# adj_resnorm on one core: x loaded once in eighths behind the first block of adj, its natural order made on TensorE in step 7

## The chip, the core and the metric

The kernel runs on one core of a Trainium2 chip. The metric is the device time of one execution, in microseconds (us); the median of three runs of the kernel before is 233.75 us (233.69 to 233.84). A separate execution was profiled, and all durations below are from it.

## The reference

There are 4096 nodes with 64 features each (x) and a 4096 x 4096 matrix adj of zeros and ones, both fp32. Two graph layers are applied, each followed by a residual sum and a layer norm.

```python
x = layernorm(x + L0(x, adj)); x = layernorm(x + L1(x, adj))
# L0: w = mask * 0.5 ** (k - pos): each neighbour weighted by its rank from the right, at most 100 of them
out = w @ (x @ weight) + bias
# L1: deg = rowsum(adj) + 1
z = concat([x, (adj @ x + x) / deg]) @ W + b
out = relu(z) / max(norm(relu(z)), 1e-12)
```

The rank of a neighbour is a running count along the row of adj (a cumulative sum), and the weights of layer 0 are powers of two of it.

## The kernel before, in words

adj is passed transposed and cut into 64 blocks of 512 rows of output by 512 neighbours: eight slabs g of rows, and in each eight blocks k of neighbours, taken from k = 7 down to 0. One such block is one step, numbered i = 8g + (7 - k) in the first slabs. A block is loaded by one DMA of POOL's queue, which turns fp32 into bf16 on the way (`load_next`, L102 to L110); eight loads are issued at the start and one more in each step, so that step i issues load i + 8. POOL waits in that instruction when eight loads are under way.

What a step does, in the order in which it is written (loop at L711): ACT's and POOL's planned work and `load_next`; `count` of the next step's block (L321, four column-tiled matmuls per block that count neighbours), whose sum DVE puts into `cs` (L331, L333); `weigh` of this step's block (L351 and L360, each sixteen 32x32-tiled matmuls into two PSUM buffers `v`), whose results ACT (L367) and DVE (L368) turn into the weights `w`; up to four sums of layer 1 for slabs whose input is ready (L387); `spread` (L339 on PE, then `near` on ACT, L341), which prepares the next step's counts; `gather` (L378, four matmuls that apply w of the step before to x). On each engine instructions run in the order in which they are written: the scheduler is manual for all engines, and the lists `hooks` and `PLACES` say which helper is put at which step and engine.

The two `v` buffers are the only ones of their pool: `weigh` of a step can begin to write when ACT and DVE have read those of the step before.

x is needed in two orders. The first order ("quads", tensor x_quads: partition = quarter e and place, column = block and q) is that of the neighbours. It lies in `xp`, which is the same memory as `c1`. `split_x` takes block k of it apart in step 7 - k into an fp16 high part (ACT for k = 7 and 6, L221, else POOL) and a rest (`xr`, POOL, L223), which DVE scales into the low part (L226, `split_x_low`) at the end of the step. `gather` and `early_px` read the fp16 parts. The second, natural order (tensor x, 128 rows to a partition block) is needed for the residual: `add_b0` (L311, POOL) adds the bias to `x1`, and `first_y` (L544) or `half_y` (L510) reads it when a slab's layer 0 ends, for slab 0 in step 9.

Before, x_quads is loaded as two halves of 512 KB on the SP queue ahead of and beside the first load of adj (L124), and x is loaded from memory a second time, 128 KB for each slab in step 8g + 3 (L128), each behind a small POOL memset that holds the trigger back (L127). The weights are loaded by the SP queue in step 1 behind a DVE memset (L213, L214), and POOL first uses them in step 5 (L229).

At the start PE runs 14 matmuls on zeros (L694) and later some on the first adj block (`warm`, L700) between the first count, spread and weigh. DVE and ACT build the constants from `dist`: `ident`, `has` and `past` (for `further`, L703 to L705), `mine` (L177, L179) and `tri` (L183, L184).

Of the kernel before, what the change touches and what calls it, by code (L numbers as in the profile page):

```python
# [9 lines left out]
F32 = mybir.dt.float32  # L10
BF16 = mybir.dt.bfloat16
# [4 lines left out]
ALU = mybir.AluOpType  # L16
# [4 lines left out]
POOL = mybir.EngineType.Pool  # L21
SP = mybir.EngineType.SP

P = 128
R = 512
TB = R // P
KB = 4
Q = P // 4
MAX_NEIGH = 100
STEP = 128.0  # L30
# [9 lines left out]
LAG = 1  # L40
SAVED = (15, 17, 18, 21, 27)
# [3 lines left out]
def adj_resnorm_kernel(  # L45
    ctx: ExitStack,
    tc: tile.TileContext,
    x: bass.AP,
# [20 lines left out]
    nc = tc.nc  # L69
    D = x.shape[2]  # L70
# [31 lines left out]
    def load_next(n=1):  # L102
        for _ in range(n):
            s = next(loads, None)
            if s is None:
                return
            g, k = s
            a = a16p.tile([P, KB, R], BF16, tag="a16", name=f"a16_{g}_{k}")
            nc.gpsimd.dma_start(out=a, in_=adjT[g, k])  # L109
            A[g][k] = a  # L110
# [11 lines left out]
    def load_xp(k0, k1):  # L122
        bs = slice(k0 * KB, k1 * KB)
        nc.sync.dma_start(out=xp[:, bs, :], in_=x_quads[:, bs, :])  # L124

    def load_x(g):
        nc.gpsimd.memset(x1[:, g * TB, 0:1], 0.0)  # L127
        nc.sync.dma_start(out=x1[:, ts(g, TB), :], in_=x[:, ts(g, TB), :])  # L128


    load_xp(NK // 2, NK)
    load_next()
    load_xp(0, NK // 2)
# [8 lines left out]
    load_next(6)  # L142
# [20 lines left out]
    nc.vector.tensor_scalar(cen, ident[0:D, 0:D], -1.0 / D, None, ALU.add)  # L163


# [8 lines left out]
    for e in range(4):  # L174
        one_hot = ident[quarters[e], quarters[e]].unsqueeze(2).to_broadcast([Q, 4 * NK, Q])
        if e % 2:
            nc.scalar.mul(mine[quarters[e]], one_hot, STEP)  # L177
        else:
            nc.vector.tensor_scalar(mine[quarters[e]], one_hot, STEP, None, ALU.mult)  # L179

    tri = const.tile([P, Q], BF16, name="tri")
    for rows in quarters:
        nc.vector.tensor_scalar(tri[rows], dist[rows, rows], 0.0, -STEP, ALU.is_lt, ALU.mult)  # L183
        nc.vector.scalar_tensor_tensor(  # L184
            tri[rows], ident[rows, rows], STEP * MAX_NEIGH, tri[rows], ALU.mult, ALU.add
        )
# [20 lines left out]
    nc.vector.tensor_copy(ident16, ident)  # L207
    ident_b = const.tile([P, P], BF16, name="ident_b")
    nc.vector.tensor_copy(ident_b, ident)
# [92 lines left out]
    def add_self(g):  # L302

        for q in range(TB):
            d = A[g][g][:, q, ts(q, P)]
            nc.gpsimd.tensor_tensor(d, d, ident_b, ALU.add)  # L306

# [300 lines left out]
    def at(i, engine, fn, *args):  # L608
        i, engine = PLACES.get(" ".join([fn.__name__, *map(str, args)]), (i, engine))
        hooks[i, engine].append((fn, args))  # L610

    def run(i, engine):
        for fn, args in hooks.pop((i, engine), []):
            fn(*args)
# [5 lines left out]
    for k in range(NK):  # L620
        i = when[0, k]
        at(i, POOL, split_x, k)
        at(i, DVE, split_x_low, k)
    at(1, DVE, load_weights)
# [3 lines left out]
    for g in range(NG):  # L628
        at(NK * g + 3, POOL, load_x, g)
        at(NK * g + 7, POOL, add_b0, g)  # L630
        at(min(NK * g + 12, NS - 2), POOL, add_self, g)
# [61 lines left out]
    for i in range(14):  # L693
        nc.tensor.matmul(pi, lhsT=idle[:, 0:P], rhs=idle, start=True, stop=True)  # L694

    def warm(n):

        a = A[0][NK - 1][:, 0, :]
        for i in range(n):
            nc.tensor.matmul(pi, lhsT=a[:, 0:P], rhs=a, start=True, stop=True)  # L700
# [6 lines left out]
    warm(4)  # L707
    spread(0, NK - 1)
    warm(2)
    held = None  # L710
    for c, chunk in enumerate(chunks):  # L711
        ahead = chunks[c + 1] if c + 1 < len(chunks) else []

        shares = [[]] * (len(chunk) - 1) + [ahead]
        nr = near[chunk[0][0]]
        for (g, k), share in zip(chunk, shares):
            i = when[g, k]
            run(i, ACT)
            load_next()
            run(i, POOL)  # L720

            w = weigh(g, k, nr) if i == 0 else None
            for s in share:
                count(*s, s == ahead[0], s == ahead[-1])
            run(i, "DVE, early")
            w = w or weigh(g, k, nr)
            run(i, "ACT, late")
            if i == 0:
                warm(4)
            n_todo = len(todo)  # L730
            done = some_sums(i, 0 if i in SAVED else QUOTA)
            half = 0
            if share and share[-1] == ahead[-1]:
                if held is not None and len(todo) == n_todo:

                    half = KB // 2
                    gather(*held, 0, half)
                spread(*ahead[-1])
            if i == 0:
                warm(3)  # L740
            if done is not None:
                evict_part(done)
            if held is not None:
                gather(*held, half)
            held = (g, k, w)
            if g > 0 and k == NK - 1:
                first_hT(g - 1)
            run(i, PE)
            run(i, DVE)
# [280 lines left out]
_INS = ["x", "x_quads", "adjT", "weights"]  # L1030
# [37 lines left out]
```

## Time and profile before

| what | value |
|---|---|
| median of three runs | 233.75 us |
| profiled execution | 233.72 us, of which 231.7 us are the span of the trace |
| PE busy | 209.5 us (90%) |
| DVE, ACT, POOL busy | 182.2, 140.6, 112.3 us |
| adj loads (64, 512 KB each as bf16) | 15.2 us median from issue to landing |
| x_quads (2 of 512 KB) | 4.5 us median |
| x, natural (8 of 128 KB) | 7.2 us median |
| weights (192.5 KB) | 7.2 us |

Times in the timeline count from the start of the span. In the timeline a row gives the start, the duration, the engine, the line, what is written and read, how many instructions were merged, and in brackets how long the engine had been idle and what ended that. PEld is the weight load of PE. In the row of groups the last two numbers are the idle time of the engine before the group and who ended most of it.

### The profile page before, as it was taken

What the parts mean: (1) busy time and instruction counts of PE and PEld (TensorE: products, weight loads), DVE (VectorE), ACT (ScalarE), POOL (GpSimd) and SP (SyncE); (2) the same over time, 40 slices, a digit from 0 to 9 for tenths busy, and PEclk for the clock granted to TensorE, in tenths of its full rate; (3) what the DMA queues carried; (4) which work ended last, traced back from release to release, by engine and by line L of the source; (5) the groups of instructions that cost most, each with busy time, mean ns of one, the idle gap of its engine ahead of it and who ended that gap; (6) DMA issues with size and microseconds to landing.
All of it is one profiled execution on the core that took longest, in us unless ns stands there. A gap on an engine that the chain in (4) does not pass through costs nothing.

```text
span 231.7 us, 7494 instructions
## 1 busy us (share of the span) xinstructions
PE 209.5 (90%) x3138; PEld 95.2 (41%) x3178; DVE 182.2 (79%) x454; ACT 140.6 (61%) x212; POOL 112.3 (48%) x211
## 2 busy tenths in 40 slices
PE   7589999998998999999999999999999999999910
PEld 2133445443533443334333433443334344776810
DVE  6459877997797789798975996687678866599983
ACT  6057886687778767686557455664675451142684
POOL 7439677761537081641584056325433040079970
PEclk9799999999999999999999999999999999999975
DMA  6999999999999999999999999999970000000013
GB/s 201 209 213 219 215 216 213 217 217 214 215 219 212 214 214 223 211 214 214 218 217 207 200 183 210 204 195 181 205 168 4 3 0 0 3 0 1 23 45 113
DMA packets 11984, 37.36 MB, mean 161 GB/s; under 512 B 1328, under 2 KB 3504, under 8 KB 11952
## 3 DMA queue, kind: packets, MB, share of 16 engines
q0 software_dynamic: 9216, 33.56, 73.7%
q1 hardware_dynamic: 2736, 3.34, 4.7%
q8 instruction: 24, 0.39, 0.6%
q14 instruction: 8, 0.07, 0.1%
HBM read 69.40 MB, written 1.05 MB: 304 GB/s over the span
## 4 chain that ended last, share of the span: by engine, by line
PE 40%; DVE 11%; POOL 4%; ACT 3%; issue 2%; ACTq 0%; DVEq 0%; POOLq 0%
PE acc L378 12%; PE acc_part L387 11%; PE v L351 5%; PE cnt L321 3%; PE v L360 3%; ACT u L961 2%; POOL scratch L947 2%; DVE w L368 2%; POOL scratch L978 2%; DVE cs L331 1%; PE rep L339 1%; PE va L930 1%; PE pz L505 1%; PE vb L387 1%; DVE part L403 1%
## 5 line engine op out<-in xcount | busy, mean ns | idle before, releaser
L367 ACT ACTIVATE w<-v,less 128x1024 int16<-128x1024 f32 x64 | 71.3, 1113 | 43.7 <-PE v L360 31.7
L368 DVE TENSOR_SCALAR w<-v 128x1024 int16<-128x1024 f32 x64 | 78.2, 1221 | 13.0 <-PE v L360 12.1
L378 PE MATMUL acc<-w,xhl 128*128 128x512 bf16 x235 | 65.2, 380 | 1.9 <-issue 1.1
L109 POOL DMA_DIRECT2D a<-in_adjT_dram x64 | 36.9, 622 | 48.2 <-PE acc_part L387 25.4
L387 PE MATMUL acc_part<-a,x1hl 128*128 128x512 bf16 x140 | 38.2, 381 | 1.8 <-issue 1.3
L378 PEld LDWEIGHTS <-xhl 128*128 128x128 f16 x256 | 23.1, 98 | 33.6 <-issue 9.7
L341 ACT ACTIVATE near<-rep,most 128x512 bf16<-128x512 f32 x40 | 27.3, 682 | 8.7 <-PE rep L339 8.6
L387 PEld LDWEIGHTS <-x1hl 128*128 128x128 f16 x224 | 18.6, 98 | 31.1 <-issue 13.3
L351 PE MATMUL v<-a,tri 32*32 32x512 bf16 x1024 | 29.6, 384 | 0.3 <-DVE w L368 0.2
L360 PE MATMUL v<-near,mine 32*32 32x512 bf16 x1024 | 28.1, 376 | 0.0
L331 DVE TENSOR_TENSOR cs<-cnt,cs 128x512 bf16<-128x512 f32 x32 | 21.9, 686 | 4.4 <-PE cnt L321 4.0
L321 PE MATMUL cnt<-a,pick 128*32 128x512 bf16 x256 | 21.4, 389 | 4.2 <-DMA a<-in_adjT_dram 2.9
L351 PEld LDWEIGHTS <-tri 32*32 32x32 bf16 x1024 | 9.5, 87 | 21.7 <-issue 21.5
L339 PE MATMUL rep<-cs,further 128*128 128x512 bf16 x40 | 15.4, 385 | 1.5 <-DVE cs L331 1.1
L565 POOL TENSOR_SCALAR x<-y,mv_l,r_l 128x64 f32<-128x64 f32 x16 | 9.1, 575 | 12.4 <-DVE dr L516 6.4
L947 POOL TENSOR_TENSOR scratch<-scratch,power 128x4 f32<-128x4 f32 (+1 forms) x5 | 6.4, 1279 | 15.2 <-DVE scratch L949 15.1
L306 POOL TENSOR_TENSOR a<-a,ident_b 128x128 bf16<-128x128 bf16 x32 | 12.7, 431 | 0.1
L321 PEld LDWEIGHTS <-pick 128*32 128x32 bf16 x256 | 5.9, 94 | 14.8 <-issue 11.3
L333 DVE CAST cs<-cnt 128x512 bf16<-128x512 f32 x8 | 5.5, 692 | 7.8 <-PE cnt L321 7.8
L360 PEld LDWEIGHTS <-mine 32*32 32x32 bf16 x1024 | 10.2, 87 | 2.8 <-issue 2.4
L961 ACT ACTIVATE u<-u,scratch 128x64 f32<-128x64 f32 x27 | 9.8, 428 | 2.2 <-POOL scratch L980 2.1
L944 ACT ACTIVATE u<-u 128x256 f32<-128x256 f32 (+1 forms) x5 | 2.5, 502 | 12.1 <-DVE u L933 12.1
(177 smaller groups left out, 272.2 us busy)
## 6 DMA issues: line engine op xcount, KB each, us to landing
a<-in_adjT_dram POOLq DMA_DIRECT2D x64, 512.0 KB, 15.2
c<-in_x_quads_dram SPq DMA_DIRECT2D x2, 512.0 KB, 4.5
x<-in_x_dram SPq DMA_DIRECT2D x8, 128.0 KB, 7.2
out_dram<-u SPq DMA_DIRECT2D x8, 128.0 KB, 1.7
wts<-in_weights_dram SPq DMA_DIRECT2D x1, 192.5 KB, 7.2
```

What stands on the lines that cost most here:

```text
L109: nc.gpsimd.dma_start(out=a, in_=adjT[g, k])
L321: nc.tensor.matmul(cnt[g][quarters[q], :], lhsT=pick[:, PW - 4 * k : PW - 4 * k + Q], rhs=A[g][k][:, q, :], start=first, stop=last,)
L331: nc.vector.tensor_tensor(new, cnt[g], cs[g], ALU.add)
L339: nc.tensor.matmul(pr, lhsT=further, rhs=cs[g], start=True, stop=True)
L341: nc.scalar.activation(near[g], pr, AF.Relu, bias=most, scale=-1.0)
L351: nc.tensor.matmul(v[e // 2][quarters[q], e % 2, :], lhsT=tri[quarters[e], :], rhs=A[g][k][quarters[e], q, :], start=True, stop=False,)
L360: nc.tensor.matmul(v[e // 2][quarters[q], e % 2, :], lhsT=mine[quarters[e], 4 * k + q, :], rhs=nr[quarters[e], :], start=False, stop=True,)
L367: nc.scalar.activation(w[:, 0:2, :], v[0], AF.Relu, bias=less)
L368: nc.vector.tensor_scalar(w[:, 2:4, :], v[1], -STEP * MAX_NEIGH, 0.0, ALU.add, ALU.max)
L378: nc.tensor.matmul(acc0[g], lhsT=xhl[:, b, :], rhs=w[:, q, :].bitcast(BF16), start=(k, q) == (NK - 1, 0), stop=(k, q) == (0, KB - 1),)
L387: nc.tensor.matmul(acc, lhsT=x1hl[:, b, :], rhs=A[g][b // KB][:, b % KB, :], start=first, stop=last)
L961: nc.scalar.activation(o[:, t, :], y[:, t, :], AF.Identity, bias=off[:, t : t + 1], scale=r[:, t : t + 1])
```

## The change

x is loaded once, only in the quads order, as eight blocks of 128 KB. The first adj load is issued ahead of them; block 7 follows at once, blocks 6 and 5 after the fifth and seventh adj loads, each behind a POOL memset, and blocks 4 to 0 in steps 0 to 4, on POOL's list behind `split_x` of that step. The natural order is made in step 7 by a new function, `natural_x`: sixteen fp32 matmuls, each of which multiplies a 32-row quarter of xp (512 columns) by a 32-wide identity `eye` and puts it at another quarter of partitions. They go into the two `v` buffers; ACT copies one of them and DVE the other into `x1`. In that step `gather` of the step before follows directly after, whole, ahead of `weigh`, and does not stand behind it as in other steps. `add_b0` of slab 0 moves from step 7 to step 8.

At the start 8 instead of 14 matmuls on zeros are run, and 1, 2, 3, 3 instead of 4, 2, 4, 3 on the first block. `tri` is built ahead of `has` and `past`; ACT makes three of the four parts of `mine` instead of two; `cen`, `ident16`, `ident_b` and the new `eye` are made behind the first `cs`.

```diff
--- before.py
+++ after.py
@@ -38,6 +38,8 @@
 HALVED = range(2, 7)
...
 LAG = 1
+WARM = 8, 1, 2, 3, 3
+NATURAL = 7
 SAVED = (15, 17, 18, 21, 27)
 
 
@@ -45,7 +47,6 @@
 def adj_resnorm_kernel(
     ctx: ExitStack,
     tc: tile.TileContext,
-    x: bass.AP,
     x_quads: bass.AP,
     adjT: bass.AP,
     weights: bass.AP,
@@ -67,7 +68,7 @@
 
 
     nc = tc.nc
-    D = x.shape[2]
+    D = x_quads.shape[2]
     NG, NK = adjT.shape[0], adjT.shape[1]
     NB = NK * KB
     NS = NG * NK
@@ -119,18 +120,14 @@
     prep = a16p.tile([P, KB * R // 2], F32, tag="a16", name="prep")
     xTs = [a16p.tile([P, KB, R], FP16, tag="a16", name=f"xT_{j}") for j in range(2)]
 
-    def load_xp(k0, k1):
-        bs = slice(k0 * KB, k1 * KB)
+    def load_xp(k, held=True):
+        bs = ts(k, KB)
+        if held:
+            nc.gpsimd.memset(xp[:, k * KB, 0:1], 0.0)
         nc.sync.dma_start(out=xp[:, bs, :], in_=x_quads[:, bs, :])
 
-    def load_x(g):
-        nc.gpsimd.memset(x1[:, g * TB, 0:1], 0.0)
-        nc.sync.dma_start(out=x1[:, ts(g, TB), :], in_=x[:, ts(g, TB), :])
-
-
-    load_xp(NK // 2, NK)
     load_next()
-    load_xp(0, NK // 2)
+    load_xp(NK - 1, False)
     dist = epi.tile([P, P], I32, tag="hT", name="dist")
     nc.gpsimd.iota(dist, [[1, P]], base=0, channel_multiplier=-1)
     load_next()
@@ -139,7 +136,11 @@
     nc.gpsimd.iota(of_p, [[4, KB], [4 * KB, NK], [1, 4]], base=0, channel_multiplier=-1)
     of_m = epi.tile([P, P], I32, tag="z", name="of_m")
     nc.gpsimd.iota(of_m, [[1, 4], [4 * KB, NK], [4, KB]], base=0, channel_multiplier=-1)
-    load_next(6)
+    load_next(3)
+    load_xp(NK - 2)
+    load_next(2)
+    load_xp(NK - 3)
+    load_next()
 
     idle = epi.tile([P, R], BF16, tag="near", name="idle")
     nc.vector.memset(idle, 0.0)
@@ -160,30 +161,29 @@
     nc.vector.tensor_scalar(ident, dist, 0.0, None, ALU.is_equal)
     cen, wcf, b0T = prep[0:D, 0:D], prep[0:D, D : 2 * D], prep[0:D, 2 * D : 4 * D]
     w32, wc32 = prep[:, 4 * D : 6 * D], prep[:, 6 * D : 7 * D]
-    nc.vector.tensor_scalar(cen, ident[0:D, 0:D], -1.0 / D, None, ALU.add)
-
-
-    has = epi.tile([P, P], BF16, tag="y", name="has")
-    nc.vector.tensor_scalar(has, of_p, 0.0, None, ALU.is_equal)
-    past = epi.tile([P, P], BF16, tag="hT", name="past")
-    nc.vector.tensor_scalar(past, of_m, 0.0, None, ALU.is_lt)
-
-    nc.scalar.activation(zero, zero, AF.Sqrt)
-
-    mine = const.tile([P, 4 * NK, Q], BF16, name="mine")
-    for e in range(4):
-        one_hot = ident[quarters[e], quarters[e]].unsqueeze(2).to_broadcast([Q, 4 * NK, Q])
-        if e % 2:
-            nc.scalar.mul(mine[quarters[e]], one_hot, STEP)
-        else:
-            nc.vector.tensor_scalar(mine[quarters[e]], one_hot, STEP, None, ALU.mult)
 
     tri = const.tile([P, Q], BF16, name="tri")
+    eye = const.tile([P, Q], F32, name="eye")
     for rows in quarters:
         nc.vector.tensor_scalar(tri[rows], dist[rows, rows], 0.0, -STEP, ALU.is_lt, ALU.mult)
         nc.vector.scalar_tensor_tensor(
             tri[rows], ident[rows, rows], STEP * MAX_NEIGH, tri[rows], ALU.mult, ALU.add
         )
+    has = epi.tile([P, P], BF16, tag="y", name="has")
+    nc.vector.tensor_scalar(has, of_p, 0.0, None, ALU.is_equal)
+    past = epi.tile([P, P], BF16, tag="hT", name="past")
+    nc.vector.tensor_scalar(past, of_m, 0.0, None, ALU.is_lt)
+
+    nc.scalar.activation(zero, zero, AF.Sqrt)
+
+    mine = const.tile([P, 4 * NK, Q], BF16, name="mine")
+    for e in range(4):
+        one_hot = ident[quarters[e], quarters[e]].unsqueeze(2).to_broadcast([Q, 4 * NK, Q])
+        if e:
+            nc.scalar.mul(mine[quarters[e]], one_hot, STEP)
+        else:
+            nc.vector.tensor_scalar(mine[quarters[e]], one_hot, STEP, None, ALU.mult)
+
     most = const.tile([P, 1], F32, name="most")
     nc.vector.memset(most, MAX_NEIGH)
     less = const.tile([P, 1], F32, name="less")
@@ -204,9 +204,7 @@
     nc.vector.memset(power, -0.5)
     x1T = const.tile([P, R], FP16, name="x1T")
     ident16 = const.tile([P, P], FP16, name="ident16")
-    nc.vector.tensor_copy(ident16, ident)
     ident_b = const.tile([P, P], BF16, name="ident_b")
-    nc.vector.tensor_copy(ident_b, ident)
 
     def load_weights():
 
@@ -304,6 +302,23 @@
         for q in range(TB):
             d = A[g][g][:, q, ts(q, P)]
             nc.gpsimd.tensor_tensor(d, d, ident_b, ALU.add)
+
+    def natural_x():
+
+        v = [ps_v.tile([P, 2, NK, D], F32, tag="v", name=f"xn_{i}") for i in range(2)]
+        quads = xp.rearrange("p (k e) m -> p k e m", e=4)
+        for q in range(KB):
+            for e in range(4):
+                nc.tensor.matmul(
+                    v[q // 2][quarters[e], q % 2, :, :],
+                    lhsT=eye[quarters[q], :],
+                    rhs=quads[quarters[q], :, e, :],
+                    start=True,
+                    stop=True,
+                )
+        to = x1.rearrange("p (k q) m -> p q k m", q=KB)
+        nc.scalar.copy(to[:, 0:2], v[0])
+        nc.vector.tensor_copy(to[:, 2:4], v[1])
 
     def add_b0(g):
 
@@ -621,13 +636,14 @@
         i = when[0, k]
         at(i, POOL, split_x, k)
         at(i, DVE, split_x_low, k)
+    for k in range(NK - 3):
+        at(NK - 4 - k, POOL, load_xp, k)
     at(1, DVE, load_weights)
     at(NK - 2, POOL, prepare)
     at(NK + 1, POOL, prepare_wx)
     at(NK + 2, POOL, prepare_wn)
     for g in range(NG):
-        at(NK * g + 3, POOL, load_x, g)
-        at(NK * g + 7, POOL, add_b0, g)
+        at(max(NK * g + 7, NATURAL + 1), POOL, add_b0, g)
         at(min(NK * g + 12, NS - 2), POOL, add_self, g)
     if HALVED:
         all_at(
@@ -690,7 +706,7 @@
 
 
     pi = ps_a.tile([P, R], F32, tag="acc1", name="pi")
-    for i in range(14):
+    for i in range(WARM[0]):
         nc.tensor.matmul(pi, lhsT=idle[:, 0:P], rhs=idle, start=True, stop=True)
 
     def warm(n):
@@ -704,9 +720,14 @@
     further = const.tile([P, P], BF16, name="further")
     nc.vector.tensor_copy(further, pf)
     count(0, NK - 1, True, True)
-    warm(4)
+    warm(WARM[1])
     spread(0, NK - 1)
-    warm(2)
+    warm(WARM[2])
+    nc.vector.tensor_scalar(cen, ident[0:D, 0:D], -1.0 / D, None, ALU.add)
+    nc.vector.tensor_copy(ident16, ident)
+    nc.vector.tensor_copy(ident_b, ident)
+    for rows in quarters:
+        nc.vector.tensor_copy(eye[rows], ident[rows, rows])
     held = None
     for c, chunk in enumerate(chunks):
         ahead = chunks[c + 1] if c + 1 < len(chunks) else []
@@ -723,24 +744,29 @@
             for s in share:
                 count(*s, s == ahead[0], s == ahead[-1])
             run(i, "DVE, early")
+            early = 0
+            if i == NATURAL:
+                natural_x()
+                early = KB
+                gather(*held)
             w = w or weigh(g, k, nr)
             run(i, "ACT, late")
             if i == 0:
-                warm(4)
+                warm(WARM[3])
             n_todo = len(todo)
             done = some_sums(i, 0 if i in SAVED else QUOTA)
             half = 0
             if share and share[-1] == ahead[-1]:
-                if held is not None and len(todo) == n_todo:
+                if held is not None and len(todo) == n_todo and not early:
 
                     half = KB // 2
                     gather(*held, 0, half)
                 spread(*ahead[-1])
             if i == 0:
-                warm(3)
+                warm(WARM[4])
             if done is not None:
                 evict_part(done)
-            if held is not None:
+            if held is not None and not early:
                 gather(*held, half)
             held = (g, k, w)
             if g > 0 and k == NK - 1:
@@ -1027,7 +1053,7 @@
         work.pop(name)()
 
 
-_INS = ["x", "x_quads", "adjT", "weights"]
+_INS = ["x_quads", "adjT", "weights"]
 
 
 def kernel(**inputs):
@@ -1040,8 +1066,7 @@
 
     a = np.asarray(arrays.pop("adj")).reshape(n // R, R, n // (KB * P), KB, P)
     arrays["adjT"] = a.transpose(0, 2, 4, 3, 1)
-    v = np.asarray(inputs["x"])
-    arrays["x"] = v.reshape(n // P, P, d).transpose(1, 0, 2)
+    v = np.asarray(arrays.pop("x"))
 
     v = v.reshape(n // (4 * P), 4, 4, P // 4, d)
     arrays["x_quads"] = v.transpose(1, 3, 0, 2, 4).reshape(P, n // P, d)
```

## Prediction

> **What bounds the kernel now.** I first asked where TensorE waits, in the profile's slices and in the table of waits, because a change of loads and start-up can only pay where the loads set the pace.
>
> ```profile
> PE   7589999998998999999999999999999999999910
> ...
> DMA  6999999999999999999999999999970000000013
> ```
>
> The DMA engines are full from 6 to 174 us, yet PE is over 90% busy too. The waits (total us, times, longest) decide between them:
>
> ```profile
> PE cnt L321 <- DMA a<-in_adjT_dram: 2.9, 2, 2.7
> ...
> PEld L321 <- DMA a<-in_adjT_dram: 1.0, 3, 0.4
> ```
>
> In 231.7 us PE waits 3 to 4 us for adj. The timeline says where: once for the first block (2.67 us, until 8.94), then for adj loads 7, 8 and 10, which are counted in steps 6, 7 and 9:
>
> ```profile
> 27.87 0.10 PEld L321 LDWEIGHTS <-pick 128*32 128x32 bf16 x4 [0.45 <-DMA a<-in_adjT_dram]
> ...
> 30.62 0.23 PEld L321 LDWEIGHTS <-pick 128*32 128x32 bf16 x4 [0.17 <-DMA a<-in_adjT_dram]
> ...
> 35.88 0.10 PEld L321 LDWEIGHTS <-pick 128*32 128x32 bf16 x4 [0.42 <-DMA a<-in_adjT_dram]
> ```
>
> So the kernel has two parts. Up to about 36 us, loads and engines run neck and neck; after that PE never waits for a load, and the chain that ended last is almost all PE from 90 to 190 us. What arrives at 36 us late or early is carried to the end one for one.
>
> The issue-to-landing times of single adj loads give the landings: load 0 at 1.23+7.7=8.93, load 1 at 2.31+9.1=11.4, load 2 at 3.65+10.2=13.85, load 4 at 4.9+13.9=18.8. Hence 2.45 us per load. Load 8, issued at 9.18, is the one that matters:
>
> ```profile
> DMA to landing us min/median/max: 21.4/21.4/21.4
> ```
>
> 9.18+21.4=30.6. Between loads 4 and 8 lie 11.8 us, 2.0 more than 4x2.45: the price of the weights and the first block of x, in flight then. Loads 13 (42.9) and 18 (55.6) are 12.7 apart with one 128 KB block of x between: 12.7-12.25=0.45 us per block. So the weights cost about 1.55.
>
> **The change, part by part.**
>
> *The start.* adj no longer queues behind 1 MB of x. Load 0 landed at 8.93. Bounds for it now: minus the 1 MB at its measured peak (the 4.0 to 5.0 us slices move about 420 GB/s: 2.5 us), plus one block (0.45), is 6.9; minus eight blocks at 0.45 plus one is 5.8. I take 6.4. Fewer warming matmuls, tri ahead of has and past, and the casts moved behind the first cs let PE follow 2 to 2.5 us earlier. If the clock starts cold that costs under 1 us, hidden as shown next.
>
> *What becomes of that gain.* The x taken out of the front comes back between the adj loads. Until load 8 lands: 8 loads, seven blocks of x, the weights: 6.4 + 8x2.45 + 7x0.45 + 1.55 = **30.7 us, against 30.6 before**. Only one block (the first natural one) is really gone by then. The engines run at 2.3 us a step (counts at 18.07, 20.34, 22.89, 25.21) and would reach step 7 at about 28, so they wait for adj. The early start is used up by step 7. The other seven natural loads (7x0.45=3.15 us of DMA) fall at 41 us and later, where nobody waits for a load: worth 0. The same holds for their memsets on POOL and triggers on SP.
>
> *natural_x, in step 7.* In PE's order it stands behind the count that waits for load 8, so the wait does not hide it. It needs block 0 of x, which is the end of a chain through POOL: each load_xp is issued behind split_x of the same step, and split_x of step s needs the block issued at step s-3. The page's DMA issues (KB, us to landing) show such loads:
>
> ```profile
> x<-in_x_dram SPq DMA_DIRECT2D x8, 128.0 KB, 7.2
> ```
>
> Block 3 goes out at step 1, after split_x of block 6, which waits for ACT's cast behind w of step 0 and near of step 1. The cast was at 16.08; 2.4 earlier it is 13.7, with 0.39 and 0.67 (xr) 14.8. It lands at 22.0; its split takes 0.41+0.79, so block 0 is issued at 23.3 and lands at 30.5 with the median 7.2, at 31.9 with the maximum 8.6. With count done at 31.1, natural_x starts at **31.3** (bounds 31.1 and 31.9). Here a rule and the row part. The Trainium skill, "DMA: Bandwidth & Descriptors", section "Anatomy of one DMA — SWDGE (gpsimd) path", fits 2.0 us + bytes/436 GB/s per DMA: an estimate of 2.3 us for 128 KB, by which block 0 lands near 20 and natural_x starts at 31.1, 0.2 earlier. I take the row: behind full adj queues the same size took 6.2 to 8.6.
>
> *Its matmuls.* No row has 32-wide fp32 matmuls of 512 columns. The near ones:
>
> ```profile
> 31.07 0.43 PE L351 MATMUL v<-a,tri 32*32 32x512 bf16 x16
> 31.30 0.42 PE L360 MATMUL v<-near,mine 32*32 32x512 bf16 x16
> 31.66 0.61 PE L378 MATMUL acc<-w,xhl 128*128 128x512 bf16 x2
> ```
>
> Thirty-two bf16 ones take 31.07 to 31.66, 0.59 us. The fp32 matmuls of L537 stand as two records each (8 for 4), so two bf16-like passes, 32 in all, bound it below by 0.59. The page "FP8 and Floating Point Precision" of the skill ("TensorE Precision Notes") gives true fp32 four passes: four sets of 16 at 0.295 are 1.2, and this rule speaks against the change. I take 1.0; by the record count alone the sum would be 0.4 smaller. Were the tiles not to overlap at all, 16x4x0.216 (the pitch of L378) is 13.8: the far end.
>
> *The copies.* Both v buffers of weigh 7 are now held by natural_x. The rows of the same size:
>
> ```profile
> L367 ACT ACTIVATE w<-v,less 128x1024 int16<-128x1024 f32 x64 | 71.3, 1113 | 43.7 <-PE v L360 31.7
> L368 DVE TENSOR_SCALAR w<-v 128x1024 int16<-128x1024 f32 x64 | 78.2, 1221 | 13.0 <-PE v L360 12.1
> ```
>
> DVE starts when the last matmul ends, 32.3, done 33.6 with hand-over. The four gathers moved ahead (4x0.22=0.87) lie under it. weigh 7 then takes 0.65: w may start at **34.25; it started at 31.89**. Queued behind w on ACT, by the pitches of before, are near 8 (1.01 later), the two small copies out of products (0.66 later), xT (0.33), w 8 (0.6) and near 9 (1.01):
>
> ```profile
> 31.89 1.11 ACT L367 ACTIVATE w<-v,less 128x1024 int16<-128x1024 f32 x1 [0.63 <-ACT xT L287]
> 32.90 0.68 ACT L341 ACTIVATE near<-rep,most 128x512 bf16<-128x512 f32 x1
> ...
> 34.91 1.12 ACT L367 ACTIVATE w<-v,less 128x1024 int16<-128x1024 f32 x1 [0.43 <-PE v L360]
> 35.92 0.68 ACT L341 ACTIVATE near<-rep,most 128x512 bf16<-128x512 f32 x1
> ```
>
> 34.25+1.01+0.66+0.33+0.6=36.85 for w 8, and 37.86 for near 9, which PE's second half of weigh 9 awaits. It was at 35.92: **1.95 us late**. About 0.4 of the 2.36 was taken up by ACT's gaps of 0.43 and less. After it PE is packed to 39.5, so nothing more is caught up; add_b0 of slab 0 (0.86 on POOL, one step later) is needed by y at 39.7 and hidden. If block 0 came too late by d, all shifts by d.
>
> *Sum.* Span 231.7 + 1.95 = 233.65; with the 2.02 us around it (233.72 less 231.7) 235.67. The profiled run stands 0.03 below the median of 233.75. I say **235.7**.
>
> **Rivals.** 0.2% (0.47 us) is about what the measurement can tell from no change.
>
> *The blocks of x queue behind each other* (0.20). Weights and first block were issued 2.2 us apart and landed 3.6 apart (25.8, 29.4). If the queue passes one such transfer per adj load, 2.45+0.45=2.9 us, eight of them from 8 us on end at 31.2 and land near 33; at 3.6 each they end at 36.8. natural_x at 33.5 gives 237.9; the splits then hold DVE too. For it: the 3.6. Against: it is one pair.
>
> *No overlap of the fp32 tiles* (0.05): 13.8 in place of 1.0, about 248. Against: L351 overlaps in the same tile shape.
>
> *Faster* (0.14). One mechanism: small blocks slip into gaps of the adj stream and cost little, so load 8 and block 0 both come early. Break-even is natural_x at 31.3-1.95=29.35. At 0.2 a block, 0.8 for weights and load 0 at 6.0, load 8 lands at 6.0+19.6+1.4+0.8=27.8; with blocks landing in 5 us block 0 lands at 14.8+5+1.2+0.1+5=26.1; the engines arrive at 28.3, so -1.0: 232.7. For it: a DMA share above 1. Against: the 2.0 us measured between loads 4 and 8.
>
> *No change* (0.09): natural_x between 28.9 and 29.8, the early start just paying for step 7.
>
> **How the numbers follow.** The likeliest, natural_x at 30.7 to 32.2, has 0.52: 235.1 to 236.6 alone. Slower 0.52+0.20+0.05=0.77, same 0.09, faster 0.14. The range from 233.6 to 238.3 takes in no change and most of the queueing case, and leaves out the faster case, the missing overlap and the tail of the queueing, about 0.2.
>
> **What would show it.** Load 0 landing near 6.4 and load 8 near 30.7; PE idle before count in steps 2 to 7, behind DMA; natural_x at 31.3 for about 1 us; weigh 7 waiting for DVE's copy; the count of load 11 about 2 us later than 39.53. Load 8 landing before 29 would make the forecast wrong on one side, block 0 landing after 33 on the other; a lag after 40 us that shrinks again would say that the rest of the kernel had slack to give.

## The result, and the profile after

The changed kernel takes 240.16 us (median of four runs, 239.68 to 240.62) against 233.72 us (233.68 to 233.84) for the kernel before in the same comparison: a ratio of 1.0277, with a 95% interval of 1.0257 to 1.0296. It is slower by 6.4 us, where 2 us were forecast, and it lies 1.9 us above the range. The profiled execution took 239.68 us, of which 237.8 are the span: 6.1 more than before.

The slices of the changed kernel:

```profile
PE   6786778999999899999999999999999999999920
...
PEclk9999979999999999999999999999999999999995
DMA  6999999999999999999999999999970000000013
```

PE's second to sixth slices, from about 6 to 36 us, now read 7, 8, 6, 7 and 7, where they read 5, 8, 9, 9 and 9 before. The sixth slice also has a granted clock of 0.7. From the eighth slice on the two rows are alike. So all of the loss should lie ahead of about 42 us.

The table of waits of the changed kernel (total us, times, longest):

```profile
POOL xhl L219 <- DMA c<-in_x_quads_dram: 9.8, 6, 4.3
...
PEld L336 <- DMA a<-in_adjT_dram: 4.9, 5, 2.2
PE cnt L336 <- DMA a<-in_adjT_dram: 3.7, 5, 1.7
DVE xhl L224 <- POOL xr L221: 3.5, 2, 2.5
```

The first row is new: POOL waits six times, 9.8 us in all, for a block of x. `split_x` starts with that wait. The last row is its heir: DVE waits for the rest `xr` that POOL makes. The two rows in the middle are the waits for adj that the forecast had: 1.0 (PEld) and 2.9 (PE) before.

PE in the timeline, first adj block to count of load 11:

```profile
6.48 0.62 PE L336 MATMUL cnt<-a,pick 128*32 128x512 bf16 x4 [0.33 <-DMA a<-in_adjT_dram]
...
19.59 0.40 PE L336 MATMUL cnt<-a,pick 128*32 128x512 bf16 x4 [1.72 <-DMA a<-in_adjT_dram]
...
25.23 0.40 PE L336 MATMUL cnt<-a,pick 128*32 128x512 bf16 x4 [0.55 <-DMA a<-in_adjT_dram]
...
30.70 0.59 PE L393 MATMUL acc<-w,xhl 128*128 128x512 bf16 x1 [1.31 <-DVE xhl L224]
...
33.44 0.62 PE L336 MATMUL cnt<-a,pick 128*32 128x512 bf16 x4
...
34.72 1.15 PE L312 MATMUL xn<-c,eye 32*32 32x512 f32 x32 [0.66 <-PE cnt L336]
...
36.96 0.81 PE L366 MATMUL v<-a,tri 32*32 32x512 bf16 x16 [0.34 <-ACT x L320]
...
45.62 0.40 PE L336 MATMUL cnt<-a,pick 128*32 128x512 bf16 x4
```

The counts of loads 6, 8 and 11 in the kernel before:

```profile
25.21 0.40 PE L321 MATMUL cnt<-a,pick 128*32 128x512 bf16 x4
...
30.75 0.40 PE L321 MATMUL cnt<-a,pick 128*32 128x512 bf16 x4
...
39.53 0.40 PE L321 MATMUL cnt<-a,pick 128*32 128x512 bf16 x4
```

Load 0 is counted at 6.48 (8.94 before). At load 4 (19.59, 20.35 before) 0.8 us of that lead is left, and at load 6 (25.23) nothing, as forecast. Load 8 landed at 31.1. Its count came at 33.44 all the same, without a wait for adj: PE had stood in `gather` at 30.70 behind DVE's fp16 part. `natural_x` then began at 34.72. The count of load 11 is at 45.62, 6.09 later than 39.53. After it nothing is lost or won: the spread of step 12 is 6.08 late (49.86 for 43.78), that of step 24 6.07 (82.22 for 76.15), that of step 38 6.02 (177.61 for 171.59).

### The profile page after: what moved, and what is told of

The parts are those of the page before. It is cut to its first block, busy times and chain, and to the rows that moved or that the text cites. A ratio compares the mean times of both kernels' runs of the same rounds, so it can differ in the third digit from the quotient of the medians.

```text
span 237.8 us, 7549 instructions
## 1 busy us (share of the span) xinstructions
PE 210.6 (89%) x3160; PEld 94.5 (40%) x3200; DVE 183.5 (77%) x458; ACT 142.7 (60%) x214; POOL 110.8 (47%) x210
## 3 DMA queue, kind: packets, MB, share of 16 engines
q0 software_dynamic: 9216, 33.56, 73.5%
q1 hardware_dynamic: 2448, 2.30, 3.3%
## 4 chain that ended last, share of the span: by engine, by line
PE 39%; DVE 10%; POOL 4%; ACT 3%; issue 2%; ACTq 0%; DVEq 0%; POOLq 0%
PE acc L393 12%; PE acc_part L402 11%; PE v L366 5%; PE cnt L336 3%; PE v L375 3%; ACT u L987 2%; POOL scratch L973 2%; DVE w L383 2%; POOL scratch L1004 1%; DVE cs L346 1%; PE rep L354 1%; PE va L956 1%; PE pz L520 1%; PE vb L402 1%; DVE part L418 1%
## 5 line engine op out<-in xcount | busy, mean ns | idle before, releaser
L383 DVE TENSOR_SCALAR w<-v 128x1024 int16<-128x1024 f32 x64 | 78.2, 1222 | 12.2 <-PE v L375 11.4
L110 POOL DMA_DIRECT2D a<-in_adjT_dram x64 | 36.3, 580 | 40.5 <-PE acc_part L402 25.8
L402 PEld LDWEIGHTS <-x1hl 128*128 128x128 f16 x224 | 18.6, 98 | 31.0 <-issue 13.3
L366 PE MATMUL v<-a,tri 32*32 32x512 bf16 x1024 | 30.2, 388 | 0.6 <-ACT x L320 0.3
## 6 DMA issues: line engine op xcount, KB each, us to landing
a<-in_adjT_dram POOLq DMA_DIRECT2D x64, 512.0 KB, 10.5
```

Of the source, the lines that this page charges most:

```text
L366: nc.tensor.matmul(v[e // 2][quarters[q], e % 2, :], lhsT=tri[quarters[e], :], rhs=A[g][k][quarters[e], q, :], start=True, stop=False,)
L383: nc.vector.tensor_scalar(w[:, 2:4, :], v[1], -STEP * MAX_NEIGH, 0.0, ALU.add, ALU.max)
L402: nc.tensor.matmul(acc, lhsT=x1hl[:, b, :], rhs=A[g][b // KB][:, b % KB, :], start=first, stop=last)
```

## What held natural_x back

The DMA issues of the changed kernel (KB each, median us from issue to landing), and the issue of block 0 alone:

```profile
c<-in_x_quads_dram SPq DMA_DIRECT2D x8, 128.0 KB, 9.6
...
wts<-in_weights_dram SPq DMA_DIRECT2D x1, 192.5 KB, 10.0
```

```profile
L127 SPq DMA_DIRECT2D c<-in_x_quads_dram x1: 328/328/328, 24.2 to 24.2; - x1
...
DMA to landing us min/median/max: 10.4/10.4/10.4
```

Block 0 was issued at 24.2 and landed at 34.6. The whole column, worked out as issue plus landing time, each rounded to 0.1:

| transfer on the SP queue | issued | took | landed | after the one before |
|---|---|---|---|---|
| block 7 | 0.7 | 2.4 | 3.1 | |
| block 6 | 5.6 | 7.7 | 13.3 | |
| block 5 | 6.8 | 9.4 | 16.2 | 2.9 |
| block 4 | 10.3 | 9.8 | 20.1 | 3.9 |
| block 3 | 14.8 | 8.2 | 23.0 | 2.9 |
| weights | 16.0 | 10.0 | 26.0 | 3.0 |
| block 2 | 17.5 | 11.4 | 28.9 | 2.9 |
| block 1 | 21.4 | 10.5 | 31.9 | 3.0 |
| block 0 | 24.2 | 10.4 | 34.6 | 2.7 |

Read the last column and not "took". From block 5 on each was issued long before the one ahead of it had landed, and they land about 3.0 us apart: (34.6-13.3)/7. In the same time the POOL queue lands one adj load (28.3, 31.1, 33.9: 2.8 each). The packets, the pieces in which the DMA engines move a transfer, show it too. From 15 to 30 us (packets, MB, share of 16 engines' time; q0 is adj's queue, q1 the SP queue):

```profile
q0 software_dynamic: 741, 2.69, 88.5%
q1 hardware_dynamic: 740, 0.74, 17.6%
```

The two queues got through the same number of packets. In the timeline POOL shows the same rhythm:

```profile
28.95 0.39 POOL L219 CAST xhl<-c 128x256 f16<-128x256 f32 x1 [4.28 <-DMA c<-in_x_quads_dram]
...
31.96 0.39 POOL L219 CAST xhl<-c 128x256 f16<-128x256 f32 x1 [0.16 <-DMA c<-in_x_quads_dram]
...
34.69 0.39 POOL L219 CAST xhl<-c 128x256 f16<-128x256 f32 x1 [1.06 <-DMA c<-in_x_quads_dram]
```

The last of these begins at 34.69 and `natural_x` at 34.72: both were released by block 0. The bracket in PE's row, "0.66 <- PE cnt", names the wrong one: the count had ended at 33.44+0.62=34.06. Where a named releaser had long been done, look for a DMA. The first row made DVE's part late by 2.48 us, which is the stall of 1.31 in `gather` at 30.70.

PE, DVE, ACT and POOL in stretches of 2 us (busy us of each, then the granted clock, DMA share and GB/s), changed kernel:

```profile
28.00:30.00 2.00, 0.98 (x36) 0.30 (x36) 0.00 (x0) 0.98 (x3) 0.96 (x2) 1.00 1.04 223
30.00:32.00 2.00, 1.30 (x4) 0.52 (x5) 1.88 (x3) 0.84 (x2) 1.61 (x5) 0.68 1.07 228
32.00:34.00 2.00, 2.00 (x12) 0.74 (x10) 0.44 (x2) 1.16 (x3) 1.54 (x3) 0.50 1.08 224
34.00:36.00 2.00, 1.34 (x37) 0.39 (x34) 0.69 (x1) 0.23 (x2) 1.23 (x3) 0.96 1.08 217
```

PE was half idle from 28 to 30. In stretches of half a microsecond the granted clock is 1.00 from 30 to 30.5, 0.73 in the next, 0.50 until 34 and 1.00 from 34.5: half speed from about 30.7 to 34.1. The count at 33.44 takes 0.62 and not 0.40; PE looks full from 32 to 34 and does half the work. The clock was back before `natural_x`, and block 0 held that to 34.6 in any case, so the slow clock should have cost little on top; no run takes it away alone.

ACT and DVE behind `natural_x`, in the timeline:

```profile
35.90 1.01 ACT L320 COPY x<-xn 128x1024 f32<-128x1024 f32 x1 [1.77 <-PE xn L312]
...
38.13 1.11 ACT L382 ACTIVATE w<-v,less 128x1024 int16<-128x1024 f32 x1 [1.22 <-PE v L375]
```

```profile
36.06 1.23 DVE L321 COPY x<-xn 128x1024 f32<-128x1024 f32 x1 [1.26 <-PE xn L312]
38.18 1.23 DVE L383 TENSOR_SCALAR w<-v 128x1024 int16<-128x1024 f32 x1 [0.90 <-PE v L375]
```

From 34.72: matmuls 1.15, hand-over to DVE 0.19, its copy 1.23, then 0.84 until both halves of `weigh` are in and w starts. That is 3.41 us from the start of `natural_x` to w of step 7; the forecast had 2.95.

## The experiments

Each was timed against the kernel before in the same session. "Halves" are two blocks of 512 KB as in the kernel before, "eighths" the eight blocks of the change.

| kernel | us | ratio to before | 95% interval |
|---|---|---|---|
| after (eighths, natural_x in step 7) | 240.16 | 1.0277 | 1.0257 to 1.0296 |
| halves, natural_x in step 7 | 236.25 | 1.0103 | 1.0073 to 1.0133 |
| eighths, all triggered at the start | 237.66 | 1.0159 | 1.0135 to 1.0183 |
| eighths, no natural_x, nothing loaded for it | 237.29 | 1.0143 | 1.0113 to 1.0173 |
| halves, no natural_x, nothing loaded for it | 235.63 | 1.0071 | 1.0049 to 1.0094 |
| eighths, natural order loaded as before | 242.42 | 1.0355 | 1.0320 to 1.0391 |
| halves, natural order loaded as before | 234.70 | 1.0040 | 1.0025 to 1.0054 |
| kernel before with natural_x in step 7 | 235.91 | 1.0077 | 1.0049 to 1.0105 |
| halves, natural_x in step 5 | 236.17 | 1.0092 | 1.0067 to 1.0117 |
| three blocks, natural_x in step 5 | 237.11 | 1.0129 | 1.0111 to 1.0147 |
| three blocks, natural order in quarters, steps 3 to 6 | 238.85 | 1.0204 | 1.0188 to 1.0220 |
| before, natural block of slab 0 in step 7 | 233.82 | 0.9992 | 0.9973 to 1.0010 |
| before, natural block of slab 0 in step 6 | 234.48 | 1.0024 | 1.0002 to 1.0046 |

**Halves in place of eighths.** The changed kernel with x in two blocks, the first behind the first adj load and the second behind the fifth.

```diff
-    load_xp(NK - 1, False)
+    load_xp(NK // 2, NK, False)
...
-    load_xp(NK - 2)
-    load_next(2)
-    load_xp(NK - 3)
-    load_next()
+    load_xp(0, NK // 2)
+    load_next(3)
...
-    for k in range(NK - 3):
-        at(NK - 4 - k, POOL, load_xp, k)
```

> The changed kernel with x in two halves of 512 KB (the first right behind the first adj load, the second behind the fifth) in place of eight blocks; natural_x stays in step 7. Theory Q (blocks of x are passed one per adj load, about 3 us each, and block 0, landing at 34.6, starts natural_x): both halves are in by about 16 us, natural_x starts at 31.2 behind the count of load 8, w of step 7 at 34.5 instead of 31.9, and 2.4 us remain of the 6.4: 236.2 us. Rival N (natural_x itself, its fp32 matmuls and its hold on the v buffers, is the loss): 240, as the changed kernel. Load 8 lands at 30 to 31 with both.

236.25: 3.9 of the 6.4 us are gone. PE in its timeline:

```profile
31.04 0.40 PE L334 MATMUL cnt<-a,pick 128*32 128x512 bf16 x4
31.37 1.14 PE L310 MATMUL xn<-c,eye 32*32 32x512 f32 x32
...
33.62 0.81 PE L364 MATMUL v<-a,tri 32*32 32x512 bf16 x16 [0.36 <-ACT x L318]
```

This is the picture that the forecast drew for the changed kernel: count at 31.04, `natural_x` at 31.37. The eighths, not the matmuls, took the larger part.

**All eighths triggered at the start.** Two readings were open: the queue passes one small transfer in 3 us, or the blocks are late because POOL issues them late. Here nothing holds a trigger back.

```diff
-    load_xp(NK - 1, False)
+    for k in reversed(range(NK)):
+        load_xp(k, False)
...
-    for k in range(NK - 3):
-        at(NK - 4 - k, POOL, load_xp, k)
```

> The changed kernel with all eight blocks of x triggered at once behind the first adj load, with no memset and no step holding them. Theory Q, with the rate of the queue as its core: the blocks land up to 3 us apart, block 0 at about 24 at the latest, so well ahead of step 7; natural_x starts at 31.2, and the time is that of the halves, 236.2 us. If instead it is the chain through POOL alone that spaces them, they land together, within 6 us, and load 0 lands at about 9 instead of 6.4; the time is then still about 236. Rival N: 240.

237.66, 1.5 more than expected. The issues of x in its trace:

```profile
L127 SPq DMA_DIRECT2D c<-in_x_quads_dram x8: 378/434/736, 0.7 to 4.6; - x8
...
DMA to landing us min/median/max: 2.4/11.0/18.8
```

The last block was issued at 4.6 and landed 18.8 us later, at 23.4; from the third on (8.9) that is (23.4-8.9)/5=2.9 us a block. So the pace is the queue's, with every trigger long past. But the second reading holds a part: block 6, triggered right behind block 7 and not at 5.6, landed at 4.4 and not 13.2, and with the weights behind the blocks and not between them the last block came 11.2 us earlier. A row of transfers is late by its pace and by when it begins. The run also parts the 3.9 us of the eighths in two. Their late arrival costs 2.5 (240.16-237.66), because here the last block comes in time. The other 1.4 (237.66-236.25) stay though no engine waits for x: load 8 landed at 31.5 and not 30.6, and `natural_x` began at 32.36 and not 31.37.

**natural_x left out.** Eighths, and in a second kernel halves. x1 is cleared by DVE and keeps nothing of x, so the residual of layer 0 lacks x; `gather` stays ahead of `weigh`.

```diff
+    at(2, DVE, clear_x1, 0, NB * 5 // 8)
+    at(4, DVE, clear_x1, NB * 5 // 8, NB)
...
-                natural_x()
```

> The changed kernel without natural_x: the sixteen matmuls and the two copies are left out, x1 is cleared by two DVE memsets in steps 2 and 4 instead, so the residual lacks x. The eight blocks stay. Theory Q: split_x of blocks 2, 1 and 0 is as late as before, the count of load 8 stays at about 33.4 (30.75 in the kernel before), and 2.7 us remain: 236.5 us. Rival N: the loss goes with natural_x, 233.7 us. Both may hold a part: between them.

> The halves without natural_x: matmuls and copies left out, x1 cleared by DVE in steps 2 and 4, so the residual lacks x. If the chain of the eight blocks (measured alone: +3.5) and natural_x (measured alone: +2.5) are separate and all there is, nothing of the loss is left: 233.4 to 234.2 us. If the start (order of the constants, fewer warming matmuls, the first adj load ahead of x) costs something of its own, it shows here as what is left above 233.7.

237.29 and 235.63: the first is 0.8 above the expected 236.5, the second 1.4 above the expected band's upper end. Neither is clean: the first clearing holds DVE for 1.12 us, and PE then waited for it (0.34 us with eighths, 0.73 with halves). With eighths PE stood 1.26 and 0.59 us in `gather` behind DVE, whose parts came late because blocks 2 and 1 landed at 29.3 and 32.1. With halves load 7 landed at 29.5, and at 28.1 in the halves with `natural_x`; no run shows why. What they can say is that the eighths are slow without `natural_x` too. For its price the next three serve better.

**The start alone: natural order loaded from memory again.** The changed start and halves, or eighths, with `load_x` and the old places of `gather` and `add_b0`.

```diff
+        at(NK * g + 3, POOL, load_x, g)
+        at(NK * g + 7, POOL, add_b0, g)
...
-                natural_x()
-                early = KB
-                gather(*held)
```

> Halves and natural order from memory: what is left of the change is the start alone (first adj load issued ahead of x, fewer warming matmuls, other order of the constants). Theory: load 8 lands at 30.6 as in the kernel before and decides: 233.5 to 234.3 us, and the halves with natural_x (236.25) less this is what natural_x costs, about 2.4. If the start itself costs something, as the last run without natural_x (235.6) could mean, it stays at 235 or more.

> The changed kernel with natural_x undone: the natural order of x is loaded from memory again, one 128 KB block per slab in step 8g+3 as in the kernel before, add_b0 and gather in their old places; the start and the eight blocks stay. A clean repeat of the run without natural_x, with nothing left out. Theory: the chain of blocks alone. Block 2 lands at 29 and block 1 at 32, and split_x of them holds gather in steps 6 and 7; the natural block of slab 0 joins the same queue and pushes the last ones back by one more place (3 us). Count of load 8 at 33 to 34; between 236.5 and 239 us. Rival N (natural_x is most of the loss): 234 us.

With halves: 234.70, 0.4 above the expected band, so the changed start alone costs 0.95 us. Its timeline:

```profile
28.87 0.40 PE L339 MATMUL cnt<-a,pick 128*32 128x512 bf16 x4 [1.26 <-DMA a<-in_adjT_dram]
...
31.74 0.40 PE L339 MATMUL cnt<-a,pick 128*32 128x512 bf16 x4
```

The engines start earlier, so the weights and the first natural block are issued 1.9 us earlier (16.7 and 19.0) and land ahead of load 7 (23.8 and 26.9), where the natural block landed between loads 7 and 8 before (29.4). Load 7 landed at 28.8 (27.8 before) and load 8 at 30.6, the same. The count of load 7 waits 1.26 us, and one step later the count of load 8 is at 31.74, where it was at 30.75: an early start brought a later step 7.

With eighths: 242.42, 3.4 above the expected band and slower than the changed kernel. The natural block of slab 0 takes one more place in the queue, and block 0 landed at 38.3. POOL, then PE:

```profile
38.37 0.39 POOL L220 CAST xhl<-c 128x256 f16<-128x256 f32 x1 [3.96 <-DMA c<-in_x_quads_dram]
...
40.14 0.34 POOL L258 COPY prep<-wts 64x128 f32<-64x128 f32 x1
```

```profile
40.54 0.61 PE L263 MATMUL pw<-prep 64*128 64x64 f32 x2 [4.60 <-POOL prep L258]
```

PE does not wait for x itself here. It waits for `bias_columns`, which stands behind the waiting `split_x` on POOL. Block 0 is 3.7 us later, one place (2.9) and 0.9 that the row had lost ahead of it; the time is 2.3 longer, although `natural_x` is gone.

**natural_x alone**, in the kernel before, with its own start and halves.

```diff
-        at(NK * g + 3, POOL, load_x, g)
-        at(NK * g + 7, POOL, add_b0, g)
+        at(max(NK * g + 7, NATURAL + 1), POOL, add_b0, g)
...
+            if i == NATURAL:
+                natural_x()
+                early = KB
+                gather(*held)
```

> The kernel before with its own start and its two halves of x in front of adj, and one part of the change: the natural order is made by natural_x in step 7 (with gather ahead of weigh, add_b0 of slab 0 in step 8) and the eight natural loads go. If the parts add (start +0.95, natural_x +1.55 where x is early, the eighths +3.9), 233.75+1.55 = 235.3 us, in 235.0 to 235.8: the natural block no longer passes ahead of load 8 (-0.45, so load 8 at about 30.2 and its count at 30.6), natural_x at about 31.0 for 1.15, near 9 about 1.5 later than 35.92. Rival: natural_x only cost time because load 8 was late, and with it 0.45 earlier the slack of ACT takes it up: 233.4 to 234.2.

235.91, 0.1 above the expected band: `natural_x` costs 2.0 us here (the kernel before had 233.88 in this comparison). The load that it saves did bring load 8 forward (30.0, was 30.6), but the weights, issued 1.2 earlier, now held load 7 to 28.1, and the count of load 8 came at 31.02. The earlier weights seem to come of the clock and not of the edit: behind the first wait for adj (2.78 us) the granted clock stayed at 1.00 in this profiled run, while it fell to 0.50 in that of the kernel before (wait 2.67 us), and load 1 was counted at 11.64 and not 12.95. The rival, that slack takes the step up, fell.

With these runs, medians in us:

| | natural order loaded | natural_x in step 7 | difference |
|---|---|---|---|
| start and halves of before | 233.88 | 235.91 | +2.0 |
| changed start, halves | 234.70 | 236.25 | +1.55 |
| changed start, eighths | 242.42 | 240.16 | -2.3 |

The parts don't add. `natural_x` costs about 1.5 to 2 us where x is early, and saves 2.3 where x is the queue that everything waits for. The middle row is no clean pair: load 0 landed at 7.3 in its first kernel and at 8.9 in its second, though both issue it in the same place, and no run shows why. The changed start makes no difference that can be told beside `natural_x` (intervals 1.0049 to 1.0105 and 1.0073 to 1.0133).

**natural_x at a better place?** Step 5, where PE waits for adj, was to hide it; with halves, and with x as 128, 384 and 512 KB. Last, a quarter of the order in each of steps 3 to 6.

```diff
-NATURAL = 7
+NATURAL = 5
```

```diff
-            if i == NATURAL:
-                natural_x()
-                early = KB
-                gather(*held)
+            if 3 <= i < 7:
+                natural_q(i - 3)
```

> As the halves, with natural_x in step 5 instead of 7, where PE waits for adj in any case. If the cost of natural_x is that it stands behind the load that sets the pace (theory), the wait for loads 7 and 8 takes it up: 233.5 to 234.2 us, and load 8, which no longer has a natural block of x ahead of it, opens step 7 at 30.3 to 30.8. If natural_x costs its 2.4 us wherever it stands: 236.2 us.

> The changed kernel with x in three transfers (block 7 at once, blocks 4 to 6 behind the third adj load, blocks 0 to 3 behind the fifth) and natural_x in step 5. Theory: three transfers are passed by about 16 us, so nothing waits for x; load 0 lands at 6.4 as in the changed kernel and PE has some 2 us of waits for adj before step 7, under which natural_x of step 5 can go. Load 8 lands near 30, its count at 30.4 (30.75 in the kernel before): 233.2 to 234.2 us. Rival (natural_x costs its 2.5 us wherever it stands, as it did in step 5 with the halves): 236.2 us.

> Loads as in the three transfers, but the natural order is made one quarter a step in steps 3 to 6: four fp32 matmuls into the bank of the early transposes, one copy of half the size (ACT, DVE, ACT, DVE), so the v buffers are not held and gather stays in its place. Theory: the fp32 matmuls are 0.3 us a step and the copies fit into ACT's and DVE's waits for adj, so load 8 alone sets step 7: 232.9 to 233.8 us. If ACT and DVE have no room in these steps: up to 1.2 us more, 234 to 235 us. Rival (natural order costs 2.5 us wherever it stands): 236.2 us.

All three missed: 236.17, 237.11 and 238.85, none below the kernel before. With halves load 0 landed at 8.8, so the engines had no lead to spend. With three blocks they had one, load 0 at 6.6, but PE waited for adj ahead of step 5 (1.27, 1.30, 0.52 and 0.22 us), and not behind it:

```profile
26.62 0.40 PE L336 MATMUL cnt<-a,pick 128*32 128x512 bf16 x4 [0.22 <-DMA a<-in_adjT_dram]
26.95 1.14 PE L312 MATMUL xn<-c,eye 32*32 32x512 f32 x32
...
30.70 0.40 PE L336 MATMUL cnt<-a,pick 128*32 128x512 bf16 x4
```

The next load had landed at 29.0 and was counted at 30.70. A load comes in 2.45 us and a step takes 2.3, so by this estimate one step can hide 0.15 us and no more. Waits that lie ahead of an instruction can't hide it. The quarters, in another PSUM buffer, waited for that buffer in three of their four steps:

```profile
29.02 0.63 PE L311 MATMUL xn<-c,eye 32*32 32x512 f32 x4 [0.63 <-ACT xT L285]
```

**A transfer less ahead of load 8**, in the kernel before: the natural block of slab 0 later.

```diff
-        at(NK * g + 3, POOL, load_x, g)
-        at(NK * g + 7, POOL, add_b0, g)
+        at(NK * g + 3 if g else 7, POOL, load_x, g)
+        at(NK * g + 7 if g else 10, POOL, add_b0, g)
```

(in the second kernel 6 and 9). In the first, `add_b0` of slab 0 comes after the y that reads x1, so that slab's residual lacks the bias.

> The kernel before, with the natural block of slab 0 loaded in step 7 rather than 3 and its add_b0 in step 10 rather than 7. If a transfer that passes between adj loads 4 and 8 is paid by the engines that wait for loads 8 and 10, 0.2 to 0.4 us are gained: 233.3 to 233.6. Rival: the block only passes later, ahead of load 10, whose count waits for it as before: 233.6 to 233.9, no change.

> The kernel before, with the natural block of slab 0 loaded in step 6 and its add_b0 in step 9, ahead of the y that reads it. The block should pass behind load 8 and land near 36.5. If the 0.33 us by which the count of load 8 came earlier with the block out of the way was lost only through POOL's work moved beside DVE's norm at 43 us, the gain stays: 233.3 to 233.6. Rival: something else takes it up, the wait for load 10 or DVE, as a start that is early finds the same next limit: 233.6 to 233.9, no change.

233.82 and 234.48: no change, and slightly slower. In both the count of load 8 came 0.3 us earlier (30.42 and 30.43, was 30.75). In the first the lead held until the count of load 12 (41.53 for 41.86) and was 0.06 by 49 us; no run shows what took it. In the second the block was under way beside load 10, which landed at 36.0 and not 35.5, so PE waited 0.37 us for it and counted it 0.13 later than before: the rival's "wait for load 10". POOL also stood at the head of step 9 for the block:

```profile
36.29 0.73 POOL L311 TENSOR_TENSOR x<-x,wts 128x256 f32<-128x256 f32 x1 [2.87 <-DMA x<-in_x_dram]
```

What is behind it (`wc_parts`, at 38.19 and not 35.10) came late for PE (0.20), and the count of load 11 was 0.31 late. No version tried is measurably faster than the kernel before.

## Why the prediction was wrong

**What bounds the kernel, and one-for-one carrying: right.** The loss stood at 6.09 us at the count of load 11 and at 6.0 to 6.1 ever after. The runs on a later natural block add that this holds for a delay; a lead of 0.3 was not kept.

**The start: right in time, wrong in worth.** Load 0 at 6.4 (6.48), load 8 at 30.7 (31.1), the lead used up before step 7: all as put. But the forecast gave the start no price, and alone it has one of 0.95 us: transfers that the engines issue earlier landed ahead of an earlier load, and that load landed 1.0 later. That the one caused the other is read from the landings and not tested apart. In the changed kernel it doesn't appear, since block 0 decides.

**Block 0, the failed step.** "Block 0 is issued at 23.3 and lands at 30.5 with the median 7.2, at 31.9 with the maximum 8.6." It was issued at 24.2 and took 10.4. The 7.2 is the median of eight natural loads. Seven of them were more than 12 us apart, each alone on its queue (6.2 to 7.9); the eighth stood behind the weights and is the 8.6. The forecast used this for blocks that stand behind one another. The same error moved the issue by 0.9: each of blocks 4 to 0 is issued behind a `split_x` that awaits an earlier one. Together 0.9+3.2=4.1, from 30.5 to 34.6. `natural_x` moved from 31.3 to 34.72, 3.4 later, as load 8 had covered the rest.

**The rule of the Trainium skill** ("DMA: Bandwidth & Descriptors", "Anatomy of one DMA — SWDGE (gpsimd) path") was set aside rightly, and not far enough. The fit is for POOL's path, and the blocks go through SP's queue. The estimate of 2.3 us for 128 KB that it gives stands against 2.4 for block 7, whose packets had nearly all begun when the first of adj did (at 2.7), and against 7.7 to 11.4 for the rest. The section "Queues, rings and completion order" of the same page, that the DMA engines take turns between queues packet by packet, is nearer to what the trace shows: 741 packets of one queue and 740 of the other in the same 15 us, one small transfer for one large. No run here changes the number of packets of a transfer, so that the turns set the pace is read from these counts and not shown by an experiment.

**natural_x and its copies.** The four-pass rule of the Trainium skill ("FP8 and Floating Point Precision", "TensorE Precision Notes"), from which the estimate of 1.2 us was worked out, was nearer than the 1.0 taken: 1.15. From there to w 2.26 were measured, 1.95 taken. In all 3.41 in place of 2.95, 0.46 too little. The catch-up behind it, put at 0.4, was 0.15, so 0.25 more.

**The sum.** 1.95 forecast, plus 3.42 for the start of `natural_x`, 0.46 and 0.25, is 6.08; 6.09 was measured at near of step 9 (42.01 for 35.92). The median lies another 0.3 higher than the forecast's allowance around the span (240.16-237.8=2.36, against 2.02).

**The rival "blocks of x queue behind each other" is what happened**, and had 0.20. Its 2.9 us per transfer was right (3.0). Its start was not: it let the queue begin at 8 us, which put block 0 "near 33"; block 6 landed only at 13.3, so eight paces of 3.04 back from 34.6 begin at 10.3. With 34.72 in its place for 33.5, and the 0.71 of the copies and the catch-up, it would have said 235.67+3.42+0.71=239.8. It was held down by "it is one pair". That pair was the only place in the trace of before with two small transfers in the queue, and so the only row with the form of the case; the seven loads alone on the queue were many, and of another form.

## What to carry to other kernels

Time from issue to landing holds what else stands in the queue: for a row of small transfers beside a full queue take the distance between two landings times their number, and not the latency of a lone one. Count packets and transfers, not bytes: here x in eight pieces took eight places, at 3 us each beside adj, and everything behind its wait on the issuing engine came late too. And before work is moved into a step because an engine waits there, look whether the wait lies behind the place or ahead of it; only a wait behind it can hide the work.

## What was not expected of the hardware

A block's size hardly changed its time beside adj. The issues of the kernel with three blocks:

```profile
c<-in_x_quads_dram SPq DMA_DIRECT2D x1, 512.0 KB, 11.9
c<-in_x_quads_dram SPq DMA_DIRECT2D x1, 384.0 KB, 9.3
...
c<-in_x_quads_dram SPq DMA_DIRECT2D x1, 128.0 KB, 2.3
```

384 KB took 9.3 us and 512 KB, next in the queue, landed 3.7 later, while 128 KB blocks took 7.7 to 11.4. The packet counts fit this. The SP queue has 2448 packets for 17 transfers in the changed kernel (eight blocks, the weights, eight outputs), 1584 for 11 with halves and 1728 for 12 with three blocks, and adj's queue 9216 for 64: 144 for each transfer, whether of 128 or of 512 KB. Where two queues get through equal numbers of packets, each transfer then costs the same place, and only its packets are larger. The larger ones are not free: beside them adj loads 2 to 4 landed 3.4 to 4.6 us apart, and 3.0 to 4.0 beside the small ones of the changed kernel.

Bytes ahead of adj are a little cheaper than between its loads: the 896 KB that the kernel before had ahead of load 0, and the changed kernel not, made it later by 2.46 us (8.94 against 6.48), which is 0.35 for each 128 KB; between loads 128 KB cost 0.45 (before).

PE's clock fell to half at about 30.7 us, after stalls of 0.79 and 1.31 us (ended at 28.41 and 30.70), with PE still busy for 0.98 of the 2 us from 28 to 30. The Trainium skill ("TensorE: Matmul & The Clock Gate", "Part 1: The HAM clock gate") has the clock fall after an idle window of some 3.4 us; here no single stall was half that long. Nor did the length of a stall decide it elsewhere: after the first wait for adj the clock fell with 2.67 us in the kernel before and stayed at 1.00 with 2.78 in the one with `natural_x` alone. What decides it stays open.
